# A graph layer on one core: 72 instead of 48 edge columns summed directly, in bf16 addends

## The chip, the cores and the metric

The kernel runs on one core of a Trainium2 chip. The metric is the device time of one execution in microseconds, as a median over runs. The core's engines are TensorE (PE, with its weight loads shown apart as PEld), VectorE (DVE), ScalarE (ACT) and GpSimd (POOL). SyncE (SP) issues transfers. Each engine takes its instructions in one order; they wait for each other through semaphores.

## The reference

There are 6250 nodes and 206,250 edges with 128 features each. `src` and `dst` hold the two ends of every edge, sorted by `dst`. The edge features are summed by `src`, so to the kernel the target of an edge is a random node.

```python
edge_aggr = jnp.zeros((n, HIDDEN)).at[src].add(edge_attr)
combined = jnp.concatenate([x, edge_aggr, global_expand], axis=-1) @ W_c + b_c
h = jax.nn.softplus(combined @ W1 + b1)
h = jax.nn.softplus(h @ W2 + b2)
out = layernorm(x + h @ W3 + b3)
```

The sum over edges, `edge_aggr`, takes nearly all of the time.

## The kernel before, in words

The edges stand as 1612 columns of 128 (the last one is short). A column holds one edge per partition. The sum is built in SBUF, transposed, as `sums_t` (128 features x 6400 nodes), in two ways.

**By scattering (1564 columns).** The columns are cut into ten groups (`GROUPS`, line 23: columns, and `sub`). For each group, `node_codes` (line 205) splits every node number into a block of 256 nodes and a place in the block. `positions` (line 243) counts, with VectorE scans and bf16 matmuls on PE, where each edge goes so that edges of one block lie together in a buffer in DRAM (`place`, three in turn). `load_rows`, `code_rows` and `scatter_rows` (lines 619 to 649) work on pieces of ten columns: SP loads the rows, ScalarE copies each edge's code beside its row (line 636), and POOL scatters each column with one indirect DMA (line 644). `reduce_steps` (line 392) then reads a finished group back in loads of eight chunks of 128 rows. VectorE makes a one-hot matrix `hot` from the codes (line 423; in the last two groups ScalarE does it for three loads in four, lines 414 to 422). PE multiplies (line 437), and VectorE adds the result to `sums_t` (line 454). `sub` chunks share one block and one add.

**Directly (48 columns).** `direct_steps` (line 545) compares the columns with every node. For 12 columns at a time (`SET`) it goes through 13 windows of 512 nodes. A job takes two columns (`QUAD`): ScalarE makes their one-hot rows in two activations and one more (lines 577 and 579), and PE multiplies in fp32 (line 589). At the end of a window, after six jobs, VectorE adds the PSUM result to `sums_t` (line 593).

**The order of the work** is written out by hand for PE, DVE, ACT and SP (lines 652 to 739). While group g is scattered, piece by piece, the steps of four lists are woven in evenly: the positions of group g+1 (done by 75% of the group), the reduction of group g-1 (by 95%), steps of the node part, and the filling of the next buffer. Direct jobs go into groups 1 to 6, shared out by `left` (line 690). All transfers keep one order as well. Lines 713 to 715 issue the rows of the third piece ahead, the codes of the second piece ahead and the scatter of the piece itself, so POOL follows what the other engines reach in their order.

**The end.** After the last reduction, an MLP runs over 13 tiles of 512 nodes. `norm` (line 814) normalises several tiles together: a Newton iteration of short VectorE operations, then a scaling of each 128-node block, on POOL or, for the last part, on VectorE. The tiles are cut into `parts` of 4, 3, 3, 2 and 1 (lines 745 to 748).

Of the kernel before, what the change touches and what calls it, by code (L numbers as in the profile page):

```python
# [16 lines left out]
P = 128  # L17
# [2 lines left out]
LOAD_COLS = 10  # L20
EPS = 1e-5

GROUPS = ((40, 1), (120, 2), (200, 4), (240, 4), (240, 4), (240, 4), (212, 4), (140, 2), (88, 2),
          (44, 1))
CHUNK_ROWS = 1024
PLACES = 3

DIRECT = 48
SET = 12
WIDE = 512  # L30
QUAD = 2
FILL = 4
POS_COLS = 20
PART_COLS = 60
# [6 lines left out]
LEAD = 3  # L41
# [6 lines left out]
def kernel(  # L48
# [36 lines left out]
    for size, sub in GROUPS:  # L85
        c1 = min(TC, c0 + size)
        if c1 > c0:
# [10 lines left out]
    dram = ctx.enter_context(tc.tile_pool(name="dram", bufs=1, space=bass.MemoryType.DRAM))  # L98


    iota_f = const.tile([P, WIDE], F32, name="iota_f")
    nc.gpsimd.iota(iota_f, pattern=[[1, WIDE]], base=0, channel_multiplier=0,
                   allow_small_or_imprecise_dtypes=True)
    part_f = const.tile([P, 1], F32, name="part_f")
    nc.gpsimd.iota(part_f, pattern=[[0, 1]], base=0, channel_multiplier=1,
# [62 lines left out]
    with ExitStack() as phase:  # L168
# [74 lines left out]
        def positions(g):  # L243
# [3 lines left out]
            steps = []  # L247
            parts = [(a, min(c1, a + PART_COLS)) for a in range(c0, c1, PART_COLS)]
            in_block, so_far, got = {}, {}, {}
            pos = per.tile([P, C_MAX], I32, name="pos")  # L250
            pos_of[g] = pos

            def by_col(t):
# [100 lines left out]
            def chunk_map():  # L354

                small = ps.tile([P, 4, P], F32, name="small", bufs=2)
                end_t = per.tile([NB, 1], F32, name="end_t")
                nc.tensor.transpose(small[:NB, 0, :], got["end"], ident)
                nc.vector.tensor_copy(end_t, small[:NB, 0, :1])
                ended = per.tile([NB, NSC_MAX], F32, name="ended")  # L360
                nc.vector.tensor_scalar(ended[:, :nsc], chunk_i[:, :nsc], end_t, None,
                                        op0=ALU.is_ge)
                offs = per.tile([1, NSC_MAX], I32, name="offs", bufs=3)
                offs_of[g] = offs
                flat = ps.tile([P, 4, P], F32, name="small", bufs=2).rearrange("p a b -> p (a b)")
                nc.tensor.matmul(flat[:1, :nsc], ones[:NB, :1], ended[:, :nsc],
                                 start=True, stop=True)
                nc.vector.tensor_scalar(offs[:, :nsc], flat[:1, :nsc], float(NB - 1), float(BL),
                                        op0=ALU.min, op1=ALU.mult)
# [22 lines left out]
        def reduce_steps(g):  # L392
# [16 lines left out]
            def match(i):  # L409
                s, k = loads[i]  # L410
                m = k * sub
                hot = hots.tile([P, CHUNK_ROWS // P, BL], F32, name="hot")
                hot_of[i] = hot
                if g > G - 3 and i % 4 != 3:

                    codes = iota_f[:, int(code_of(g)):int(code_of(g)) + BL]
                    for j in range(m):
                        nc.scalar.activation(hot[:, j], codes, AF.Abs,  # L418
                                             bias=chunks[i][:, j, D:W], scale=-1.0)
                    nc.scalar.activation(hot[:, :m], hot[:, :m], AF.Relu, bias=ones[:, :1],  # L420
                                         scale=-1.0)
                    return
                nc.vector.scalar_tensor_tensor(  # L423
                    hot[:, :m], chunks[i][:, :m, D:W].to_broadcast([P, m, BL]),
                    code_of(g), iota_ps.unsqueeze(1).to_broadcast([P, m, BL]),
                    op0=ALU.subtract, op1=ALU.is_equal)
# [118 lines left out]
        def direct_steps():  # L545


            steps = []
            if not ND:
                return steps  # L550
            NW = -(-NB * BL // WIDE)
            less = keep.tile([P, NW, ND], F32, name="less")
            rows_in, hot_of, sum_of = {}, {}, {}

            def begin():

                first = keep.tile([P, NW], F32, name="first")
                nc.gpsimd.iota(first, pattern=[[WIDE, NW]], base=0, channel_multiplier=0,
                               allow_small_or_imprecise_dtypes=True)
                part, node, _ = whole_nodes(0, ND)  # L560
                nc.vector.tensor_copy(node, part)
                nc.vector.tensor_tensor(
                    less, node.unsqueeze(1).to_broadcast([P, NW, ND]),
                    first.unsqueeze(2).to_broadcast([P, NW, ND]), op=ALU.subtract)

            def load(c):
                n = min(SET, ND - c)
                rows_in[c] = direct_p.tile([P, SET, D], F32, name="direct_rows", bufs=2)
                sync_dma(rows_in[c][:, :n],
                         edge_attr[:P * T, :].rearrange("(p t) d -> p t d", p=P)[:, c:c + n, :])  # L570

            def compare(c, w, q):
                n = min(WIDE, NB * BL - w * WIDE)
                hot = direct_p.tile([P, QUAD, WIDE], F32, name="direct_hot", bufs=4)
                hot_of[c, w, q] = hot
                for j in range(QUAD):
                    nc.scalar.activation(hot[:, j, :n], iota_f[:, :n], AF.Abs,  # L577
                                         bias=less[:, w, c + q + j:c + q + j + 1], scale=-1.0)
                nc.scalar.activation(hot[:, :, :n], hot[:, :, :n], AF.Relu, bias=ones[:, :1],  # L579
                                     scale=-1.0)  # L580

            def add(c, w, q):
                n = min(WIDE, NB * BL - w * WIDE)
                k = min(SET, ND - c)
                hot = hot_of.pop((c, w, q))
                if q == 0:
                    sum_of[c, w] = ps.tile([P, WIDE], F32, name="direct_sum", bufs=2)
                for j in range(QUAD):
                    nc.tensor.matmul(sum_of[c, w][:, :n], rows_in[c][:, q + j, :], hot[:, j, :n],  # L589
                                     start=(q + j == 0), stop=(q + j == k - 1))  # L590
                if q + QUAD == k:
                    here = sums_t[:, w * WIDE:w * WIDE + n]
                    nc.vector.tensor_add(here, here, sum_of.pop((c, w))[:, :n])  # L593

            jobs = [(c, w, q) for c in range(0, ND, SET) for w in range(NW)
                    for q in range(0, min(SET, ND - c), QUAD)]
            steps += [begin, lambda: load(0)]
            for i in range(len(jobs) + 2):
                def one(i=i):
                    if i < len(jobs):  # L600
                        c, w, q = jobs[i]
                        if (w, q) == (NW // 2, 0) and c + SET < ND:
                            load(c + SET)
                        compare(*jobs[i])
                    if i > 1:
                        add(*jobs[i - 2])
                steps.append(one)
            return steps
# [23 lines left out]
        def code_rows(i):  # L632
            if i >= len(pieces):
                return
            g, c, k, r = pieces[i]
            nc.scalar.copy(rows_at[i][:r, :k, D:W], low[:r, c:c + k].unsqueeze(2))  # L636

        def scatter_rows(i):
            g, c, k, r = pieces[i]
# [12 lines left out]
        with tc.manual_schedule(engines={ET.PE, ET.DVE, ET.Activation, ET.SP}):  # L652
# [35 lines left out]


            left = [0.0] * G  # L690
            for g in range(1, G - 3):
                left[g] = max(0.0, groups[g][1] - groups[g][0]
                              - groups[g - 1][3] * groups[g - 1][2] / 3 - (9 if 3 <= g < 6 else 0))
            direct_at = 0.0
            i = 0
            assert G > 6
            nodes = []
            for g in range(G):
                mine = [q for q in range(len(pieces)) if pieces[q][0] == g]
                prep = []  # L700
                if g + 1 < G:
                    prep = [lambda g=g: node_codes(*groups[g + 1][:2])] + positions(g + 1)
                sums = reduce_steps(g - 1) if g else []

                if g == 3:
# [4 lines left out]
                filled = fill_rows(g + 1)  # L710
                done = [0, 0, 0, 0]
                for q in mine:
                    load_rows(i + LEAD)
                    code_rows(i + LEAD - 1)
                    scatter_rows(i)
                    i += 1

# [26 lines left out]

    tiles = [(n0, min(4 * P, N - n0)) for n0 in range(0, N, 4 * P)]
    order = tiles[-1:] + tiles[:-1]
    parts = [order[:4]] + [order[i:i + 3] for i in range(4, len(order) - 3, 3)]
    parts += [order[len(parts) * 3 + 1:-1], order[-1:]]
    h1, h2, sub_z, x_of = {}, {}, {}, {}

    def blocks(w):
# [62 lines left out]
    def norm(now, last):  # L814
# [9 lines left out]
        for _ in range(3):  # L824
            nc.vector.tensor_mul(t, g, g)
            nc.vector.scalar_tensor_tensor(t, t, -0.5, v, op0=ALU.mult, op1=ALU.mult)
            nc.vector.scalar_tensor_tensor(g, t, 1.5, g, op0=ALU.add, op1=ALU.mult)  # L827

        engine = nc.vector if last else nc.gpsimd
        for n0, w, y, at in now["done"]:  # L830
            for lo, hi, r in blocks(w):
                for q in range(lo, hi):
                    engine.tensor_scalar(y[:r, q, :], y[:r, q, :], mv[:r, at + q, 0:1],  # L833
                                         rs[:r, 1, at + q:at + q + 1],
                                         op0=ALU.subtract, op1=ALU.mult)
                m0 = n0 + lo * P
                sync_dma(
                    out[m0:m0 + (hi - lo) * r, :].rearrange("(b p) d -> p b d", p=r),
# [58 lines left out]
```

## Time and profile before

| what | value |
|---|---|
| median of 3 runs | 2163.2 us (2162.69 to 2173.22) |
| profiled execution | 2166.67 us, span 2164.9 us |
| first to last scatter on POOL | 25.6 to 2019.3 us |
| from the last scatter to the first MLP matmul | 66.7 us |
| from there to the end | 78.9 us |
| busy: PE, DVE, ACT, POOL | 1789.7, 1328.0, 912.7, 1560.2 us |
| mean granted clock of PE | 0.925 |

In a group's row of the profile, "out<-in xcount" is followed by the busy time, the mean duration of one instruction in nanoseconds, and the idle time of the engine before them with what ended it. An fp32 matmul appears as two instructions. Matmuls overlap, so the time of one is read from the starts of neighbours rather than from its duration. The chain follows the work that ended last back from the end.

### The profile page before, as it was taken

How to read it: one execution, taken by the hardware profiler on the slowest of the kernel's cores; microseconds unless marked ns; L12 is line 12 of the kernel's file. 1: busy time of each engine (PE TensorE's matmuls, PEld its weight loads, DVE VectorE, ACT ScalarE, POOL GpSimd, SP SyncE). 2: the span in 40 equal slices, each digit the busy share in tenths (PEclk: the TensorE clock that was granted, in tenths of full speed). 3: DMA queues.
4: the chain of work that ended last, by engine and by line, in shares of the span. 5: the costliest groups of instructions: out<-in, count | busy, mean ns of one | idle time of the engine just before them, and what ended most of it. 6: DMA issues, size and time to landing. Idle time of an engine off the chain costs nothing.

```text
span 2164.9 us, 22230 instructions
## 1 busy us (share of the span) xinstructions
PE 1789.7 (83%) x6415; PEld 1209.0 (56%) x6415; DVE 1328.0 (61%) x1923; ACT 912.7 (42%) x1350; POOL 1560.2 (72%) x1631
## 2 busy tenths in 40 slices
PE   3398788966889878999889998788998899688884
PEld 0144445534555555666556666556666778566752
DVE  7386457524656345675465855355755798796567
ACT  0476665653444335444353443353342000006964
POOL 5777777777777767777777777777777777777226
PEclk8699999987999999999999999999999999899997
DMA  9998788738786665676756666556766687776521
GB/s 299 303 313 270 216 256 251 231 101 262 213 225 189 194 193 148 188 207 188 198 173 180 194 190 175 169 167 189 202 198 170 211 245 227 214 213 199 151 75 60
DMA packets 415376, 435.50 MB, mean 201 GB/s; under 512 B 37743, under 2 KB 305766, under 8 KB 415254
## 3 DMA queue, kind: packets, MB, share of 16 engines
q1 hardware_dynamic: 365062, 330.71, 54.9%
q0 software_dynamic: 50048, 103.35, 14.4%
q8 instruction: 51, 0.84, 0.2%
q14 instruction: 71, 0.58, 0.1%
q10 hardware_dynamic: 144, 0.02, 0.0%
HBM read 260.90 MB, written 173.03 MB: 200 GB/s over the span
## 4 chain that ended last, share of the span: by engine, by line
PE 57%; DVE 15%; POOL 9%; issue 7%; DMA 6%; ACT 4%; DVEq 1%; SPq 0%; POOLq 0%; ACTq 0%
PE part L437 37%; PE direct_sum L589 16%; POOL place L644 8%; DVE hot L423 7%; DMA place<-rows,pos 4%; DVE sums_t L454 2%; ACT hot L418 2%; DVE so_far L316 1%; DVE sums_t L593 1%; DMA rows<-in_edge_attr 1%; DMA chunks<-place 1%; PE small L339 1%; POOL y L833 1%; DVEq L448 1%; DVE pos L350 1%
## 5 line engine op out<-in xcount | busy, mean ns | idle before, releaser
L644 POOL DMA_INDIRECT place<-rows,pos x1564 | 1503.2, 961 | 509.0 <-issue 443.5
L437 PE MATMUL part<-hot,chunks 128*128 128x256 f32 x4472 | 1106.0, 405 | 267.8 <-DVE hot L423 250.9
L437 PEld LDWEIGHTS part<-hot,chunks 128*128 128x128 f32 x4472 | 894.9, 203 | 507.8 <-DVE hot L423 310.5
L577 ACT ACTIVATE direct_hot<-iota_f,less 128x512 f32<-128x512 f32 (+1 forms) x624 | 404.6, 695 | 811.0 <-PE direct_sum L589 808.1
L423 DVE SCALAR_TENSOR_TENSOR hot<-chunks,iota_ps 128x2048 f32<-128x2048 f32 (+1 forms) x261 | 592.2, 2270 | 44.2 <-DMA chunks<-place 44.2
L589 PE MATMUL direct_sum<-direct_hot,direct_rows 128*128 128x512 f32 (+1 forms) x1248 | 559.0, 580 | 29.4 <-DMA direct_rows<-in_edge_attr 25.6
L454 DVE TENSOR_TENSOR sums_t<-sums_t,part 128x256 f32 x781 | 327.1, 419 | 133.3 <-PE part L437 110.8
L589 PEld LDWEIGHTS direct_sum<-direct_hot,direct_rows 128*128 128x128 f32 x1248 | 233.3, 190 | 232.2 <-issue 204.9
L579 ACT ACTIVATE direct_hot<-direct_hot,ones 128x1024 f32<-128x1024 f32 (+1 forms) x312 | 348.0, 1115 | 10.1
L593 DVE TENSOR_TENSOR sums_t<-sums_t,direct_sum 128x512 f32<-128x512 f32 (+1 forms) x52 | 34.7, 667 | 410.5 <-PE direct_sum L589 410.5
L636 ACT COPY rows<-src_i 128x10 f32<-128x10 f32 (+1 forms) x159 | 30.7, 196 | 360.3 <-DMA place<-rows,pos 328.9
L350 DVE TENSOR_REDUCE pos<-at 128x20 int32<-128x500 f32 (+2 forms) x80 | 87.0, 1087 | 2.7
L316 DVE TENSOR_TENSOR_SCAN so_far<-iota_ps,ib 128x1500 bf16<-128x1500 f32 (+5 forms) x29 | 85.7, 2955 | 0.0
L418 ACT ACTIVATE hot<-iota_f,chunks 128x256 f32<-128x256 f32 x156 | 64.2, 493 | 26.7 <-DMA chunks<-place 24.2
L845 POOL TENSOR_TENSOR x_sb<-x_sb,b_all 128x512 f32<-128x512 f32 (+1 forms) x13 | 15.2, 1219 | 67.8 <-DMA x_sb<-in_x 67.8
L348 DVE TENSOR_TENSOR at<-small,ib 128x500 f32<-128x500 f32 (+2 forms) x80 | 52.9, 661 | 4.2 <-PE small L339 3.5
L833 POOL TENSOR_SCALAR y<-y,mv,rs 128x128 f32<-128x128 f32 (+1 forms) x45 | 35.2, 796 | 19.9 <-DVE rs L827 19.0
L262 DVE TENSOR_TENSOR ib<-block,iota_ps 128x1500 bf16<-128x1500 bf16 (+5 forms) x29 | 44.2, 1550 | 0.0
L273 PE MATMUL small<-ib,ones_h 128*128 128x500 bf16 (+2 forms) x80 | 23.8, 406 | 23.9 <-DVE ib L262 23.9
L536 DVE TENSOR_SCALAR z_x<-small,z_bias 128x512 f32<-128x512 f32 (+1 forms) x13 | 9.3, 718 | 51.3 <-PE small L534 51.3
L335 PE MATMUL small<-so_far,ones_h 128*128 128x500 bf16 (+2 forms) x80 | 31.4, 393 | 11.1 <-DVE last L319 11.1
L420 ACT ACTIVATE hot<-hot,ones 128x2048 f32<-128x2048 f32 (+1 forms) x20 | 39.2, 1960 | 0.7
(115 smaller groups left out, 472.7 us busy)
## 6 DMA issues: line engine op xcount, KB each, us to landing
chunks<-place SPq DMA_DIRECT2D x278, 516.0 KB, 4.5
rows<-in_edge_attr SPq DMA_DIRECT2D x155, 640.0 KB, 6.7
place<-fill SPq DMA_DIRECT2D x252, 258.0 KB, 8.3
place<-rows,pos POOLq DMA_INDIRECT x1564, 4.5
x_sb<-in_x SPq DMA_DIRECT2D x24, 256.0 KB, 4.6
direct_rows<-in_edge_attr SPq DMA_DIRECT2D x4, 768.0 KB
out<-y SPq DMA_DIRECT2D x12, 256.0 KB, 2.2
chunks<-place SPq DMA_DIRECT2D x3, 258.0 KB, 3.2
```

What stands on the lines that cost most here:

```text
L316: nc.vector.tensor_tensor_scan(t, iota_ps[:, 1:2].to_broadcast([P, NB * n]), in_block[k][0], 0.0, op0=ALU.mult, op1=ALU.add)
L350: nc.vector.tensor_reduce(pos[:, a - c0 + j0:a - c0 + j1], at.rearrange("p b g -> p g b"), axis=mybir.AxisListType.X, op=ALU.add)
L418: nc.scalar.activation(hot[:, j], codes, AF.Abs, bias=chunks[i][:, j, D:W], scale=-1.0)
L423: nc.vector.scalar_tensor_tensor(hot[:, :m], chunks[i][:, :m, D:W].to_broadcast([P, m, BL]), code_of(g), iota_ps.unsqueeze(1).to_broadcast ...
L437: nc.tensor.matmul(part[:, s - q, :], t[:, s * sub + j, :D], hot[:, s * sub + j], start=(j == 0), stop=(j == sub - 1))
L454: nc.vector.tensor_add(here, here, part[:, s - q, :])
L577: nc.scalar.activation(hot[:, j, :n], iota_f[:, :n], AF.Abs, bias=less[:, w, c + q + j:c + q + j + 1], scale=-1.0)
L579: nc.scalar.activation(hot[:, :, :n], hot[:, :, :n], AF.Relu, bias=ones[:, :1], scale=-1.0)
L589: nc.tensor.matmul(sum_of[c, w][:, :n], rows_in[c][:, q + j, :], hot[:, j, :n], start=(q + j == 0), stop=(q + j == k - 1))
L593: nc.vector.tensor_add(here, here, sum_of.pop((c, w))[:, :n])
L644: s = nc.gpsimd.indirect_dma_start(out=dst, out_offset=bass.IndirectOffsetOnAxis(ap=at, axis=0), in_=rows[:r, j, :], in_offset=None)
L833: engine.tensor_scalar(y[:r, q, :], y[:r, q, :], mv[:r, at + q, 0:1], rs[:r, 1, at + q:at + q + 1], op0=ALU.subtract, op1=ALU.mult)
```

## The change

Four parts. First, 72 columns are summed directly. Their fp32 values are split exactly into three bf16 addends: VectorE takes the upper half of each number, then the upper half of the rest, then what is left. PE multiplies three bf16 matmuls per column and window in place of one fp32 matmul. The one-hot rows become bf16, with three buffers in place of four. The first load of direct rows comes a little earlier. Second, the groups after the sixth are cut anew: 178, 116, 84, 44, 24 and 14 columns in place of 212, 140, 88 and 44, and the last four have `sub` 1. ScalarE's one-hot work covers the last four groups (`TAIL`), and in the last three POOL copies the codes itself (`late`). Third, from group 5 on the positions are computed two groups ahead (`SOONER`). Fourth, the last three MLP tiles share one norm, whose scaling is split between VectorE and ScalarE.

```diff
-GROUPS = (... (212, 4), (140, 2), (88, 2), (44, 1))
+GROUPS = (... (178, 4), (116, 2), (84, 1), (44, 1), (24, 1), (14, 1))
+SOONER = 5
+TAIL = 4
-DIRECT = 48
+DIRECT = 72
+SPLIT = 2
...
-            pos = per.tile([P, C_MAX], I32, name="pos")
+            pos = per.tile([P, C_MAX], I32, name="pos", bufs=3)
...
-                if g > G - 3 and i % 4 != 3:
+                if g >= G - TAIL and i % 4 != 3:
...
+            def halves(t):
+                return [t.bitcast(BF16).rearrange("p c (d h) -> p c d h", h=2)[:, :, :, h]
+                        for h in (0, 1)]
+
+            def split(c):
+                n = min(SET, ND - c)
+                less = less_of[c] = direct_p.tile([P, NW, SET], F32, name="less", bufs=2)
+                nc.vector.tensor_tensor(
+                    less[:, :, :n], node_f[:, c:c + n].unsqueeze(1).to_broadcast([P, NW, n]),
+                    first.unsqueeze(2).to_broadcast([P, NW, n]), op=ALU.subtract)
+                low_in[c] = direct_p.tile([P, SET, D], BF16, name="direct_low", bufs=2)
+                for a in range(0, min(SET, ND - c), SPLIT):
+                    b = min(a + SPLIT, SET, ND - c)
+                    rest = direct_p.tile([P, SPLIT, D], F32, name="direct_rest")[:, :b - a]
+                    x_c = rows_in[c][:, a:b]
+                    nc.vector.tensor_sub(rest, x_c, halves(x_c)[1])
+                    nc.vector.tensor_sub(low_in[c][:, a:b], rest, halves(rest)[1])
+                    nc.vector.tensor_copy(halves(x_c)[0], halves(rest)[1])
...
-                hot = direct_p.tile([P, QUAD, WIDE], F32, name="direct_hot", bufs=4)
+                hot = direct_p.tile([P, QUAD, WIDE], BF16, name="direct_hot", bufs=3)
...
-                for j in range(QUAD):
-                    nc.tensor.matmul(sum_of[c, w][:, :n], rows_in[c][:, q + j, :], hot[:, j, :n],
-                                     start=(q + j == 0), stop=(q + j == k - 1))
+                for j in range(q, q + QUAD):
+                    addends = halves(rows_in[c][:, j:j + 1]) + [low_in[c][:, j:j + 1]]
+                    for i, part in enumerate(addends):
+                        nc.tensor.matmul(sum_of[c, w][:, :n], part[:, 0], hot[:, j - q, :n],
+                                         start=(j == 0 and i == 0), stop=(j == k - 1 and i == 2))
...
-            steps += [begin, lambda: load(0)]
+            steps += [lambda: load(0), begin, lambda: split(0)]
...
                         if (w, q) == (NW // 2, 0) and c + SET < ND:
                             load(c + SET)
+                        if (w, q) == (NW - 2, 0) and c + SET < ND:
+                            split(c + SET)
...
-            nc.scalar.copy(rows_at[i][:r, :k, D:W], low[:r, c:c + k].unsqueeze(2))
+            copy = nc.gpsimd.tensor_copy if late(i) else nc.scalar.copy
+            copy(rows_at[i][:r, :k, D:W], low[:r, c:c + k].unsqueeze(2))
+
+        def late(i):
+            return i < len(pieces) and pieces[i][0] > G - TAIL
...
-                if g + 1 < G:
-                    prep = [lambda g=g: node_codes(*groups[g + 1][:2])] + positions(g + 1)
+                for k in range(g + 1 + (g > SOONER), min(G, g + 2 + (g >= SOONER))):
+                    prep += [lambda k=k: node_codes(*groups[k][:2])] + positions(k)
...
                     load_rows(i + LEAD)
-                    code_rows(i + LEAD - 1)
+                    if not late(i + LEAD - 1):
+                        code_rows(i + LEAD - 1)
+                    if late(i):
+                        code_rows(i)
                     scatter_rows(i)
...
-    parts = [order[:4]] + [order[i:i + 3] for i in range(4, len(order) - 3, 3)]
-    parts += [order[len(parts) * 3 + 1:-1], order[-1:]]
+    parts = [order[:4]] + [order[i:i + 3] for i in range(4, len(order), 3)]
...
+                    if last and q % 2:
+                        nc.scalar.activation(y[:r, q, :], y[:r, q, :], AF.Identity,
+                                             bias=minus[:r, k:k + 1], scale=g[:r, k:k + 1])
+                        continue
```

More of the change, by code (lines that the diff above doesn't have):

```diff
@@ L21 @@
 EPS = 1e-5
-GROUPS = ((40, 1), (120, 2), (200, 4), (240, 4), (240, 4), (240, 4), (212, 4), (140, 2), (88, 2),
-          (44, 1))
+GROUPS = ((40, 1), (120, 2), (200, 4), (240, 4), (240, 4), (240, 4), (178, 4), (116, 2), (84, 1), (44, 1),
+          (24, 1), (14, 1))
+SOONER = 5
+TAIL = 4
 CHUNK_ROWS = 1024
 PLACES = 3
-DIRECT = 48
+DIRECT = 72
 SET = 12
@@ L98 @@
     dram = ctx.enter_context(tc.tile_pool(name="dram", bufs=1, space=bass.MemoryType.DRAM))
-    iota_f = const.tile([P, WIDE], F32, name="iota_f")
-    nc.gpsimd.iota(iota_f, pattern=[[1, WIDE]], base=0, channel_multiplier=0,
+    iota_f = const.tile([P, TAIL * BL], F32, name="iota_f")
+    nc.gpsimd.iota(iota_f, pattern=[[1, TAIL * BL]], base=0, channel_multiplier=0,
                    allow_small_or_imprecise_dtypes=True)
@@ L362, in chunk_map @@
                                         op0=ALU.is_ge)
-                offs = per.tile([1, NSC_MAX], I32, name="offs", bufs=3)
+                offs = per.tile([1, NSC_MAX], I32, name="offs", bufs=4)
                 offs_of[g] = offs
@@ L551, in direct_steps @@
             NW = -(-NB * BL // WIDE)
-            less = keep.tile([P, NW, ND], F32, name="less")
-            rows_in, hot_of, sum_of = {}, {}, {}
+            node_f = keep.tile([P, ND], F32, name="node_f")
+            first = keep.tile([P, NW], F32, name="first")
+            less_of = {}
+            rows_in, low_in, hot_of, sum_of = {}, {}, {}, {}
             def begin():
-                first = keep.tile([P, NW], F32, name="first")
                 nc.gpsimd.iota(first, pattern=[[WIDE, NW]], base=0, channel_multiplier=0,
                                allow_small_or_imprecise_dtypes=True)
[L560 to L564, printed above, removed]
+                part, _, _ = whole_nodes(0, ND)
+                nc.vector.tensor_copy(node_f, part)
             def load(c):
@@ L577, in compare @@
                     nc.scalar.activation(hot[:, j, :n], iota_f[:, :n], AF.Abs,
-                                         bias=less[:, w, c + q + j:c + q + j + 1], scale=-1.0)
+                                         bias=less_of[c][:, w, q + j:q + j + 1], scale=-1.0)
                 nc.scalar.activation(hot[:, :, :n], hot[:, :, :n], AF.Relu, bias=ones[:, :1],
@@ L690 @@
             left = [0.0] * G
-            for g in range(1, G - 3):
+            for g in range(1, G - TAIL - 1):
                 left[g] = max(0.0, groups[g][1] - groups[g][0]
                               - groups[g - 1][3] * groups[g - 1][2] / 3 - (9 if 3 <= g < 6 else 0))
+            direct_first = direct[:1]
+            direct = direct[1:]
             direct_at = 0.0
@@ L712 @@
                 for q in mine:
+                    if g == 0 and q == mine[-1]:
+                        for step in direct_first:
+                            step()
                     load_rows(i + LEAD)
-                    code_rows(i + LEAD - 1)
+                    if not late(i + LEAD - 1):
+                        code_rows(i + LEAD - 1)
+                    if late(i):
+                        code_rows(i)
                     scatter_rows(i)
@@ L827, in norm @@
             nc.vector.scalar_tensor_tensor(g, t, 1.5, g, op0=ALU.add, op1=ALU.mult)
-        engine = nc.vector if last else nc.gpsimd
+        if last:
+            minus = work.tile([P, 16], F32, name="minus")[:, :nb]
+            nc.vector.scalar_tensor_tensor(minus, mv[:, :nb, 0], -1.0, g,
+                                           op0=ALU.mult, op1=ALU.mult)
         for n0, w, y, at in now["done"]:
@@ L832, in norm @@
                 for q in range(lo, hi):
-                    engine.tensor_scalar(y[:r, q, :], y[:r, q, :], mv[:r, at + q, 0:1],
-                                         rs[:r, 1, at + q:at + q + 1],
-                                         op0=ALU.subtract, op1=ALU.mult)
+                    k = at + q
+                    if last and q % 2:
+                        nc.scalar.activation(y[:r, q, :], y[:r, q, :], AF.Identity,
+                                             bias=minus[:r, k:k + 1], scale=g[:r, k:k + 1])
+                        continue
+                    (nc.vector if last else nc.gpsimd).tensor_scalar(
+                        y[:r, q, :], y[:r, q, :], mv[:r, k, 0:1], g[:r, k:k + 1],
+                        op0=ALU.subtract, op1=ALU.mult)
                 m0 = n0 + lo * P
```

## The prediction

> **What bounds the kernel now.** I read the page's chain and groups first, then the busy time of each engine in each scatter group, then the timeline around the longest PE waits, and last the spacing of bf16 matmuls.
>
> ```profile
> PE 57%; DVE 15%; POOL 9%; issue 7%; DMA 6%; ACT 4%; DVEq 1%; SPq 0%; POOLq 0%; ACTq 0%
> ...
> L644 POOL DMA_INDIRECT place<-rows,pos x1564 | 1503.2, 961 | 509.0 <-issue 443.5
> L437 PE MATMUL part<-hot,chunks 128*128 128x256 f32 x4472 | 1106.0, 405 | 267.8 <-DVE hot L423 250.9
> ...
> L577 ACT ACTIVATE direct_hot<-iota_f,less 128x512 f32<-128x512 f32 (+1 forms) x624 | 404.6, 695 | 811.0 <-PE direct_sum L589 808.1
> ...
> L579 ACT ACTIVATE direct_hot<-direct_hot,ones 128x1024 f32<-128x1024 f32 (+1 forms) x312 | 348.0, 1115 | 10.1
> L593 DVE TENSOR_TENSOR sums_t<-sums_t,direct_sum 128x512 f32<-128x512 f32 (+1 forms) x52 | 34.7, 667 | 410.5 <-PE direct_sum L589 410.5
> ```
>
> POOL scatters without a pause: 0.961 us and 0.30 of issue, one each 1.265 us, from 25.6 to 2019.3. So it looks like the bound; yet the chain is 57% PE, and PE waits 250.9 us for VectorE's `hot`. In the next view a row is one scatter group (groups 1 to 6, those with direct work); the columns are length, then busy time and instructions of PE, PE's weight load, DVE, ACT and POOL, then the granted PE clock.
>
> ```profile
> 81.20:232.80 151.60, 129.96 (x372) 63.16 (x372) 91.95 (x147) 107.52 (x144) 115.34 (x120) 0.96 0.95 276
> 232.80:485.90 253.10, 203.06 (x636) 121.89 (x636) 132.22 (x185) 147.59 (x206) 192.19 (x201) 0.91 0.73 217
> 485.90:789.60 303.70, 246.57 (x840) 165.47 (x841) 156.87 (x182) 117.60 (x168) 230.59 (x241) 0.88 0.73 209
> 789.60:1102.30 312.70, 279.74 (x985) 187.56 (x983) 183.42 (x215) 135.11 (x186) 230.61 (x240) 0.95 0.67 190
> 1102.30:1405.90 303.60, 264.64 (x966) 181.78 (x966) 181.51 (x215) 127.71 (x183) 230.51 (x240) 0.96 0.63 181
> 1405.90:1675.30 269.40, 240.63 (x878) 167.72 (x879) 161.35 (x194) 107.20 (x154) 203.65 (x212) 0.97 0.64 184
> ```
>
> PE is 80 to 90% busy here, and its clock falls below 1 wherever it paused. How much slack is left? I paired ScalarE's n-th copy of codes (L636) with the n-th piece of ten scatters: the copy stood 45 us ahead of its scatter at the start of group 2, 48 at group 3, then 2, 5, 11 and 13 at the starts of groups 4 to 7. All engines but POOL follow one written order, so that order passed the six starts at 188, 438, 788, 1098, 1395 and 1662, and needed 250, 350, 310, 297 and 267 us for groups 2 to 6. POOL alone needs 253, 304, 304, 304 and 268. **The ordered engines are as slow as POOL; the stage has two bounds, and no slack after group 3.** What they lose time to:
>
> ```profile
> 677.26 0.69 DVE L593 TENSOR_TENSOR sums_t<-sums_t,direct_sum 128x512 f32<-128x512 f32 x1 [14.04 <-PE direct_sum L589]
> 677.87 0.67 DVE L348 TENSOR_TENSOR at<-small,ib 128x500 f32<-128x500 f32 x1
> 678.57 1.10 DVE L350 TENSOR_REDUCE pos<-at 128x20 int32<-128x500 f32 x1
> ...
> 679.58 2.29 DVE L423 SCALAR_TENSOR_TENSOR hot<-chunks,iota_ps 128x2048 f32<-128x2048 f32 x1
> ...
> 681.93 4.63 PE L437 MATMUL part<-hot,chunks 128*128 128x256 f32 x10 [4.70 <-DVE hot L423]
> ```
>
> At each closing of a 512-node window VectorE stands in L593 until PE has finished the window; only then does it make the next `hot`, and PE has nothing to do: 4.70 us here. Closings and PE waits come in pairs through the groups.
>
> **The change, part by part.** *Fewer scatters*: 24 x 1.265 = 30.4 us off POOL. *More direct work*: a job (two columns, one window) is four fp32 matmul instructions at 0.43 us = 1.72 us of PE now (901.86 to 903.58 in PE's timeline); it becomes six bf16 ones. The trace has bf16 matmuls of nearly that size, each with its own weight load:
>
> ```profile
> 903.58 0.38 PE L334 MATMUL small<-ib,upto_h 128*128 128x500 bf16 x1
> 903.79 0.37 PE L335 MATMUL small<-so_far,ones_h 128*128 128x500 bf16 x1
> 904.01 0.37 PE L336 MATMUL small<-more,ones_h 128*128 128x500 bf16 x1
> 904.31 0.38 PE L339 MATMUL small<-begin,scale_h 2*128 2x500 bf16 x1
> ```
>
> They start 0.21 to 0.22 us apart (0.30 where the moving operand is broadcast), so a job is 6 x 0.2155 = 1.29 us. Here a rule of the Trainium skill speaks otherwise: TensorE: Matmul & The Clock Gate, section Back-to-back issue gap, gives about 131 ns for a matmul of 512 columns in a stream with weight loads. By it a job is 0.79 us and 403 jobs (groups 2 to 6) cost 202 us less than by the row. I take the row: same engine, same kernel. 312 jobs become 468. Counted in the two orders, group by group: jobs 42, 64, 58, 53, 53, 44 become 67, 100, 92, 82, 83, 46. With sums, positions and node steps at their durations PE's work changes by +16, +16, +21, +11, +22, -18 us. (Group 5 also takes the positions of group 7; group 6 is 34 columns shorter for POOL, not for PE.)
>
> *More closings*: 52 become 78. For each I took VectorE's work from L593 to the next match less PE's work in between: for groups 2 to 6 that gives 22, 43, 16, 21, 28 us now (measured PE gaps 36, 72, 33, 37, 31, with 9 and 24 of the first two waiting for the first transfer) and 28, 41, 41, 37, 29 in the new order: +6, -1, +25, +16, +1. *Clock*: the same page, section Part 1: The HAM clock gate, says the clock halves after an idle window of 3.4 us and returns after a busy one. The trace agrees in kind: 0.88 where the 4.7 us gaps lie, 0.97 in group 6. Applied to the new gaps that is -8, +8, +10, +6 us in groups 3 to 6; without the rule, nothing. It speaks against the change.
>
> *ScalarE*: a job stays 2 x 0.65 + 1.115, or 2.41 us. 64 jobs of group 1, after PE's first matmul, last 154 us of ScalarE: the order starts group 2 at about 218 (its first copy stands two pieces ahead), not 188: +30. bf16 output alone saves nothing. Three `hot` buffers instead of four cost nothing from group 3 on, where a job comes every 3.3 to 3.7 us; in group 2 (2.5 us apart) up to 15, inside the range.
>
> *Splitting*: per 12 columns 19 VectorE operations, 12 of them two-input ones like L199 (0.37 at 200 elements, so 0.42 at 256), 6 copies at about 0.3, one `less`: 7 us. It stands one job ahead of a closing, so VectorE has no lead to cover it; half shows: 5 x 3 = +15. *Early direct load*: it now passes one load of rows on SP; 768 KB at 300 GB/s, +2.6 us of POOL before group 2, +0 behind a stage bound by PE.
>
> Group 3 loses 20 us of waiting for its first transfer, as the order no longer runs ahead. Sum for the order: 30 + 22 - 8 + 44 + 48 - 11 + 15 = +140, so it passes the start of group 7 at 1662 + 140 = 1802, POOL 4 us later at 1806. POOL alone would be there at 84 + 1218 x 1.265 = 1625: **it waits 181 us, against about 9 now.** Positions two groups ahead don't help: POOL is held by codes and rows, which stand in the order of ScalarE and SP.
>
> *After group 7's start*: 282 columns x 1.265 = 356.7. Eleven copies now on POOL: between a POOL iota of 13 elements (0.14) and ScalarE's copy plus issue (0.5), near the latter: +4. *Tail*: the last 262 128-row chunks all have sub 1. The last group now, also sub 1, took 41.0 us for 68 chunks (2043.0 to 2084.1), 0.603 each; 262 take 158, starting 9 us after group 8's last scatter, while 82 columns and the copies take 108: 58 us from the last scatter to the MLP, against 66.7. *Shared norm*: one Newton chain of 12 short VectorE operations (2148.27 to 2150.95) goes, twelve normalisations are split over two engines instead of eight on POOL and four on VectorE: -2, of a stage of 78.9.
>
> 1806 + 356.7 + 4 + 58 + 76.9 = 2302 us of span. The profiled execution had 2164.9 of span (2166.67 in all), the median of the runs is 2163.2; taking the same 1.7 off gives **2300**.
>
> **Rivals.** *PE's waits do not multiply* (two jobs after a closing hide the match, the split is covered): the order gains only 30 + 16 + 1 + 11 + 22 - 18 = 62, POOL's group 7 starts at 1728, the end is at 2222. For it: with more jobs between matches PE has more cover. Against: the count above already takes that cover off.
> *Faster*: PE's job is far cheaper than the row says, as the skill's 131 ns would have it. Then POOL alone is the bound: 2164.9 - 30.4 + 2.6 + 4 - 8.7 - 2 = 2130, or 2129. It decides at the place where the order must pass group 7 by 1665: 137 us less over 403 jobs, 0.34 a job, a spacing under 0.16 us. Against it stand three rows at 0.21.
> *Weight loads show*: the halves are read with a step of two elements; if that spaces the matmuls as L339's 0.305, 403 x 6 x 0.09 = 217 more, 2516. Against: fp32 loads of 0.19 us hide behind 0.215 now.
>
> **How the numbers follow.** Main case 0.60 (own range 2240 to 2370), waits not multiplied 0.20, faster 0.13, weight loads 0.05, between these (no change) 0.02. Range 2190 to 2390: it leaves out faster, no change and weight loads, 0.20 together. A difference under 0.5% can't be told from none. Faster 0.13, same 0.02, slower 0.85.
>
> **What would show it.** POOL scatters no longer each 1.265 us in groups 2 to 6: some 150 us of waits for ScalarE's copies or rows; group 7 starts near 1800; L437 waits for VectorE's `hot` about 60 us longer; direct matmuls 0.21 apart; the first group's jobs at ScalarE's 2.4 us. Wrong if POOL keeps its pace through group 5, or if VectorE no longer stands in the window's add.

## The result, and the profile after

The changed kernel takes 2300.6 us (median of 4 runs, 2294.0 to 2304.9). Beside it the kernel before took 2163.5 us. The ratio is 1.062, with a 95% interval of 1.058 to 1.066. The forecast was 2300 us.

These are the chain and the groups of the changed kernel that answer to the rows shown of before.

```profile
PE 55%; DVE 18%; DMA 8%; ACT 7%; issue 5%; POOL 4%; SPq 1%; DVEq 1%; ACTq 0%; POOLq 0%
...
L682 POOL DMA_INDIRECT place<-rows,pos x1540 | 1477.5, 959 | 676.7 <-issue 421.2
L443 PE MATMUL part<-hot,chunks 128*128 128x256 f32 x4476 | 1125.9, 410 | 248.6 <-DVE hot L429 226.2
...
L605 ACT ACTIVATE direct_hot<-iota_f,less 128x512 bf16<-128x512 f32 (+1 forms) x936 | 604.9, 693 | 631.6 <-PE direct_sum L619 629.1
L619 PE MATMUL direct_sum<-direct_hot,direct_rows 128*128 128x512 bf16 (+1 forms) x1872 | 540.5, 372 | 100.0 <-ACT direct_hot L607 64.9
...
L607 ACT ACTIVATE direct_hot<-direct_hot,ones 128x1024 bf16<-128x1024 bf16 (+1 forms) x468 | 521.9, 1115 | 15.2
...
L623 DVE TENSOR_TENSOR sums_t<-sums_t,direct_sum 128x512 f32<-128x512 f32 (+1 forms) x78 | 52.0, 667 | 516.2 <-PE direct_sum L619 515.8
```

POOL has 24 scatters fewer, at the same 959 ns. Yet it now idles 676.7 us, against 509.0 before, and its share of the chain fell from 9% to 4%. VectorE stands 515.8 us before the window's add, against 410.5. The chain of waits says whom POOL waits for; its columns are the time in all, how often, and the longest wait.

```profile
POOL place L644 <- ACT rows L636: 12.3, 7, 9.3
...
POOL place L682 <- ACT rows L670: 189.0, 50, 13.2
```

The first row is the kernel before, the second the changed one. The wait grew by 177 us, a little more than the loss of 137 us and the 30.4 us of spared scatters together.

Groups 1 to 6 of the changed kernel, in the same columns as the stages of before:

```profile
86.00:237.60 151.60, 124.58 (x518) 63.39 (x519) 95.58 (x156) 130.17 (x173) 115.30 (x120) 0.98 1.00 275
237.90:516.30 278.40, 230.32 (x1004) 134.98 (x1003) 151.91 (x230) 231.84 (x323) 192.53 (x200) 0.95 0.72 201
516.60:855.50 338.90, 279.86 (x1190) 180.90 (x1190) 175.06 (x223) 217.14 (x297) 230.04 (x240) 0.93 0.68 190
864.40:1197.80 333.40, 282.89 (x1225) 188.00 (x1224) 188.56 (x233) 195.97 (x269) 229.89 (x240) 0.95 0.61 169
1205.30:1543.40 338.10, 288.81 (x1268) 191.59 (x1266) 206.52 (x274) 194.87 (x268) 230.23 (x240) 0.95 0.57 162
1545.30:1799.30 254.00, 227.06 (x977) 164.29 (x977) 148.52 (x180) 117.09 (x162) 170.42 (x178) 0.94 0.64 178
```

POOL is busy for the same 230 us in each group of 240 columns, but such a group now lasts 333 to 339 us instead of 304 to 313. Between some rows lie stretches in which POOL stood before a group's first scatter, 19 us in all. With them, the time from group 2's first scatter to group 7's grew from 1442.5 to 1561.8 us, by 119. PE's busy time grew by 87 us of these (1234.9 to 1321.9), its idle time by 32 (207.6 to 239.9). POOL's group 7 starts at 1799.7, against 1675.6 before.

### The profile page after: what moved, and what is told of

It reads as the page before. It is cut to its first block, busy times and chain, and to the rows that moved or that the text cites. A ratio compares the mean times of both kernels' runs of the same rounds, so it can differ in the third digit from the quotient of the medians.

```text
span 2303.1 us, 26251 instructions
## 1 busy us (share of the span) xinstructions
PE 1884.3 (82%) x7985; PEld 1254.2 (54%) x7985; DVE 1417.7 (62%) x2201; ACT 1302.7 (57%) x1869; POOL 1530.4 (66%) x1610
## 4 chain that ended last, share of the span: by engine, by line
PE 55%; DVE 18%; DMA 8%; ACT 7%; issue 5%; POOL 4%; SPq 1%; DVEq 1%; ACTq 0%; POOLq 0%
PE part L443 37%; PE direct_sum L619 14%; DVE hot L429 7%; DVE sums_t L460 5%; DMA place<-rows,pos 4%; POOL place L682 4%; DMA place<-fill 3%; ACT direct_hot L605 3%; ACT direct_hot L607 2%; SPq L151 1%; DVE sums_t L623 1%; DVE so_far L322 1%; DMA chunks<-place 1%; ACT hot L424 1%; DVE pos L356 1%
## 5 line engine op out<-in xcount | busy, mean ns | idle before, releaser
L682 POOL DMA_INDIRECT place<-rows,pos x1540 | 1477.5, 959 | 676.7 <-issue 421.2
L443 PE MATMUL part<-hot,chunks 128*128 128x256 f32 x4476 | 1125.9, 410 | 248.6 <-DVE hot L429 226.2
L443 PEld LDWEIGHTS part<-hot,chunks 128*128 128x128 f32 x4476 | 902.0, 206 | 460.4 <-DVE hot L429 264.5
L605 ACT ACTIVATE direct_hot<-iota_f,less 128x512 bf16<-128x512 f32 (+1 forms) x936 | 604.9, 693 | 631.6 <-PE direct_sum L619 629.1
L619 PE MATMUL direct_sum<-direct_hot,direct_rows 128*128 128x512 bf16 (+1 forms) x1872 | 540.5, 372 | 100.0 <-ACT direct_hot L607 64.9
L429 DVE SCALAR_TENSOR_TENSOR hot<-chunks,iota_ps 128x2048 f32<-128x2048 f32 x255 | 578.5, 2270 | 2.0 <-DMA chunks<-place 2.0
L607 ACT ACTIVATE direct_hot<-direct_hot,ones 128x1024 bf16<-128x1024 bf16 (+1 forms) x468 | 521.9, 1115 | 15.2
L623 DVE TENSOR_TENSOR sums_t<-sums_t,direct_sum 128x512 f32<-128x512 f32 (+1 forms) x78 | 52.0, 667 | 516.2 <-PE direct_sum L619 515.8
L619 PEld LDWEIGHTS <-direct_rows 128*128 128x128 bf16 x1872 | 180.2, 98 | 310.0 <-issue 106.8
L619 PE MATMUL direct_sum<-direct_hot,direct_low 128*128 128x512 bf16 (+1 forms) x936 | 347.7, 371 | 0.0
L619 PEld LDWEIGHTS <-direct_low 128*128 128x128 bf16 x936 | 91.5, 98 | 103.4 <-issue 1.1
L356 DVE TENSOR_REDUCE pos<-at 128x20 int32<-128x500 f32 (+3 forms) x80 | 85.5, 1068 | 2.7
L322 DVE TENSOR_TENSOR_SCAN so_far<-iota_ps,ib 128x1500 bf16<-128x1500 f32 (+7 forms) x29 | 84.5, 2912 | 0.0
L354 DVE TENSOR_TENSOR at<-small,ib 128x500 f32<-128x500 f32 (+3 forms) x80 | 52.2, 652 | 5.4 <-PE small L345 4.8
```

The costliest lines, as they stand in the source:

```text
L322: nc.vector.tensor_tensor_scan(t, iota_ps[:, 1:2].to_broadcast([P, NB * n]), in_block[k][0], 0.0, op0=ALU.mult, op1=ALU.add)
L354: nc.vector.tensor_mul(at, got.pop((k, j0)), in_block[k][1][:, :, j0:j1])
L356: nc.vector.tensor_reduce(pos[:, a - c0 + j0:a - c0 + j1], at.rearrange("p b g -> p g b"), axis=mybir.AxisListType.X, op=ALU.add)
L429: nc.vector.scalar_tensor_tensor(hot[:, :m], chunks[i][:, :m, D:W].to_broadcast([P, m, BL]), code_of(g), iota_ps.unsqueeze(1).to_broadcast ...
L443: nc.tensor.matmul(part[:, s - q, :], t[:, s * sub + j, :D], hot[:, s * sub + j], start=(j == 0), stop=(j == sub - 1))
L605: nc.scalar.activation(hot[:, j, :n], iota_f[:, :n], AF.Abs, bias=less_of[c][:, w, q + j:q + j + 1], scale=-1.0)
```

## The experiments

Two theories stood against each other. The first is that of the prediction: PE, DVE, ACT and SP follow one written order, that order became slower than POOL, and what makes it slow is PE's added work together with VectorE standing in the window's add. The rival: the new resources cost the time, that is, three one-hot buffers instead of four, and the splitting.

### Four parts of the changed kernel, one at a time

A fourth buffer for the one-hot rows (one buffer of `x_t`, used by the node part, makes room):

```diff
-x_ts[b0] = per.tile([P, 4 * P], F32, name="x_t")
+x_ts[b0] = per.tile([P, 4 * P], F32, name="x_t", bufs=1)
-hot = direct_p.tile([P, QUAD, WIDE], BF16, name="direct_hot", bufs=3)
+hot = direct_p.tile([P, QUAD, WIDE], BF16, name="direct_hot", bufs=4)
```

> The changed kernel with four buffers of one-hot rows in place of three (room for it from a single x_t buffer). PE waits 54 us in groups 2 to 6 for ScalarE's one-hot rows, a wait that was nearly absent before. Theory (the written order is too long because of PE's work and the closings): at most half of that wait goes, 2275 to 2300 us. Rival (ScalarE, held by three buffers, is the cause): the wait and what follows from it go, 2240 us or less.

The window's add written three jobs later, when PE has long finished the window:

```diff
 if q + QUAD == k:
-    here = sums_t[:, w * WIDE:w * WIDE + n]
-    nc.vector.tensor_add(here, here, sum_of.pop((c, w))[:, :n])
+    closing.append((c, w, n))
+if q == 2 * QUAD or (c + SET >= ND and w == NW - 1 and q + QUAD == k):
+    close()      # the same two lines, for each window in `closing`
```

> The changed kernel with the add of a finished window written three jobs later, so that VectorE no longer stands in it. Theory, with closings as a large term: PE's waits for VectorE's matches in groups 2 to 6, 180 us now, fall below 80, the half clock with them, and the order loses 100 to 150 us: 2150 to 2200 us. Rival (PE's own work is all that makes the order long; the waits would only move elsewhere): above 2270 us.

48 direct columns, with all other parts of the change kept (bf16 addends, short last groups, positions, norm):

```diff
-(178, 4), ... DIRECT = 72
+(202, 4), ... DIRECT = 48
```

> The changed kernel with 48 direct columns again (group 6 gets the 24 back), all other parts kept. Theory: the order is as long as before the change or shorter, POOL keeps its 1.265 us per scatter to group 7, which starts at 1655 to 1670, and 503 us follow: 2158 to 2175 us. Rival (the bf16 form itself, with its splits, or the new copies on POOL slow the kernel): above 2200 us.

No splitting: VectorE's three operations on each pair of columns go, the upper half of each number is multiplied three times, and the two lower addends are left out of the sums. Of this edit the diff shows the matmuls' part.

```diff
-addends = halves(rows_in[c][:, j:j + 1]) + [low_in[c][:, j:j + 1]]
+addends = [halves(rows_in[c][:, j:j + 1])[1]] * 3
```

> The changed kernel without the splitting on VectorE: the upper half of each value is multiplied three times, so PE does the same work and the sums are left inexact. Theory (half of the 7 us per split shows): 10 to 25 us less, 2275 to 2290 us. Rival (VectorE's bursts are the main cause): 60 us less or more, 2240 us or below.

| kernel | time, us | POOL's group 7 starts | POOL waits for ScalarE's copies |
|---|---|---|---|
| changed | 2300.6 | 1799.7 | 189.0 |
| four one-hot buffers | 2270.6 | 1767.5 | 156.8 |
| add three jobs later | **2127.2** | 1625.3 | 0.6 |
| 48 direct columns | 2162.2 | 1658.0 | 5.0 |
| no splitting | 2291.9 | 1786.8 | 178.8 |

The four variants ran once each, beside 2163.6 us of the kernel before; the changed kernel's own four runs lie 11 us apart. The fourth buffer is worth 30 us and the splitting about 9, which one run can hardly tell from nothing, so the resources don't carry the loss. With 48 columns all of it is gone (2162.2): the other parts together come out at nothing, and the 24 columns cost 138 us although they take 30.4 us of scatters off POOL. The late add alone brings 173 us, and its group 7 starts at 1625.3, the time the prediction gave for POOL alone (1625). Only the run with 48 columns fell into the range that the first theory named. The fourth buffer gained 4 us more than its range, the missing splits 2 us less, and the late add 23 us more; all three lie nearer to that theory than to the rival.

The two timelines show why. The first is the changed kernel at a closing; the columns are the start, the length, the instruction, and the idle time ahead of it with what ended it. PE's weight loads and some rows are left out.

```profile
959.69 0.38 PE L619 MATMUL direct_sum<-direct_hot,direct_low 128*128 128x512 bf16 x1
...
960.10 1.33 ACT L605 ACTIVATE direct_hot<-iota_f,less 128x512 bf16<-128x512 f32 x2 [2.27 <-PE direct_sum L619]
960.10 0.69 DVE L623 TENSOR_TENSOR sums_t<-sums_t,direct_sum 128x512 f32<-128x512 f32 x1 [10.07 <-PE direct_sum L619]
...
960.71 2.28 DVE L429 SCALAR_TENSOR_TENSOR hot<-chunks,iota_ps 128x2048 f32<-128x2048 f32 x1
...
963.04 3.72 PE L443 MATMUL part<-hot,chunks 128*128 128x256 f32 x16 [2.03 <-DVE hot L429]
```

VectorE, with the next one-hot tile still to make, stands 10.07 us in the add until PE's last direct matmul; then PE stands 2.03 us until that tile is made. The second is the version with the late add:

```profile
953.28 0.69 DVE L616 TENSOR_TENSOR sums_t<-sums_t,direct_sum 128x512 f32<-128x512 f32 x1
...
953.67 0.38 PE L627 MATMUL direct_sum<-direct_hot,direct_rows 128*128 128x512 bf16 x1
953.89 2.28 DVE L429 SCALAR_TENSOR_TENSOR hot<-chunks,iota_ps 128x2048 f32<-128x2048 f32 x1
```

Here the add waits for nothing, and the tile is made while PE multiplies the next window. Over groups 2 to 6, VectorE stands 129.1 us before the add instead of 486.5.

### The late add again, and in the kernel before

> The changed kernel with each window's add written three jobs later, once more for an interval: the last time the kernel before itself took 2863.5 us on that chip, with PE's weight loads standing 480.8 us for nothing that the profile names. Where the kernel before takes its 2163 us, the ratio should be 0.983 (0.980 to 0.986). Where the engines stand as they did then, the written order is the bound in both kernels, and the 68 us of PE work that 24 columns add should make it slower: 1.02 to 1.04, as then.

The same edit in the kernel before:

> The kernel before with the deferred add alone, once more. Theory as before: where POOL keeps its pace of 1.265 us in it, 2154 to 2163 us, ScalarE's copies at the start of group 7 more than 30 us ahead of their scatters instead of 13. Rival, that the closings cost the kernel before itself dearly: under 2130 us. Where the engines stand as in the last call: 0.98 again, for there the order is the bound.

Both came as expected for a kernel before of 2163 us. Beside 2162.3 us of the kernel before, on the same chip, the changed kernel with the late add took 2130.0 us (ratio 0.9845, interval 0.9825 to 0.9866), and the kernel before with the late add 2155.5 us (0.9964, 0.9951 to 0.9977). The latter has these waits:

```profile
ACT rows L645 <- DMA place<-rows,pos: 576.7, 84, 18.3
...
DVE hot L423 <- DMA chunks<-place: 311.0, 58, 41.8
```

ScalarE and VectorE now stand waiting for scatters and for scattered rows: the order has run ahead of POOL. The copies stand 34 to 49 us ahead of their scatters at the starts of groups 2 to 7, where before it was 2 to 11 at groups 4 to 7. That gains only POOL's 9 us of waits and costs it nothing: where POOL is the bound, a lighter order is worth nearly nothing. In the changed kernel, with its 24 columns more, the same edit is worth 171 to 173 us. Together the changes beat both kernels, by 32 us against before.

The stages of the changed kernel with the late add are POOL's own 303 us per 240 columns, and PE is busy 91% of them (1258.5 of 1388.7 us in groups 2 to 6, idle 130.2 instead of 239.9). Rows of its groups show what is left:

```profile
L691 POOL DMA_INDIRECT place<-rows,pos x1540 | 1478.1, 960 | 499.4 <-issue 432.8
L443 PE MATMUL part<-hot,chunks 128*128 128x256 f32 x4476 | 1052.3, 390 | 141.9 <-DVE hot L429 112.8
...
L627 PE MATMUL direct_sum<-direct_hot,direct_rows 128*128 128x512 bf16 (+1 forms) x1776 | 519.5, 371 | 100.7 <-ACT direct_hot L607 67.7
```

PE's waits for VectorE's tiles halved (226.2 to 112.8). Those for ScalarE's tiles stayed (64.9 and 67.7); they don't hold up POOL here.

### Six runs on chips where the engines paused

Six runs fell on two chips where the kernel before itself took 2863.5 and 2870.4 us. Its late-add version shows the pauses in the chain of waits:

```profile
ACT direct_hot L577 <- remote: 716.2, 59, 37.5
POOL place L653 <- ACT rows L645: 541.1, 68, 19.6
...
DVE sums_t L454 <- remote: 531.1, 49, 39.2
...
PE part L437 <- issue: 272.9, 179, 12.4
```

"Remote" and "issue" mean that the wait ended with nothing that this core's profile shows; in the run of the same kernel shown above, PE's, VectorE's and ScalarE's instructions have no such wait. A scatter is as long as there (958 and 961 ns). What holds the engines is not known; the DMA packets that bring the instructions take as long as there (0.68 and 0.69 us on average), so these don't tell it. POOL waits 541.1 us for copies, so there the written order is the bound even in this kernel. These runs can be read against each other only.

> The changed kernel with each window's add written three jobs later, as before, for an interval. One look gave 2127.2 us, so the ratio to the kernel before should be 0.983, with an interval that stays under 0.99. If the one look was a lucky one: 1.00.

> The kernel before with the deferred add alone. Theory: the closings cost the written order time there as well, but that order and POOL were level, POOL waited only about 9 us in all, and its scatters set the end, so 2154 to 2163 us, with the copies 30 us and more ahead of their scatters at the start of group 7 instead of 13. Rival, that the closings cost the kernel before itself dearly (its PE waited 250.9 us for the one-hot tiles): under 2130 us, and deferral is no answer to what the change added.

Against the kernel before, the late-add version of the change came to 1.033 (1.026 to 1.041), and the late-add version of before to 0.984 (0.975 to 0.994). Both misses fit the first theory: where the order is the bound, the late add helps the kernel before by 45 us, and the change with its 24 columns costs 119 us (2937.5 against 2818.9) though the add is late in both. That is an explanation after the result; no expectation had it. The gain of the changed version thus hangs on the order being faster than POOL.

The last groups of before (188, 140, 88 and 44 columns) in the late-add version, on both chips:

```diff
-(178, 4), (116, 2), (84, 1), (44, 1), (24, 1), (14, 1)   TAIL = 4
+(188, 4), (140, 2), (88, 2), (44, 1)                     TAIL = 2
```

> The same, but with the four last groups of the kernel before (188, 140, 88 and 44 columns, ScalarE copying all codes) in place of the six short ones. The scatters are as many. The prediction's step (a tail of 58 us after the last scatter with short groups, 66.7 with long ones, 4 us of copies on POOL) makes this 5 us slower: 2132 us. My reading of the changed kernel's trace (its tail is 68 us, so the short groups shorten nothing, and the copies on POOL cost 4): 2122 us. Short groups worth what their shape suggests (half the last group's reduction, some 20 us): 2145 us or more.

> The deferred version with the four last groups of the kernel before (188, 140, 88 and 44 columns, ScalarE copying all codes) in place of the six short ones, once more. The scatters are as many. The deferred version itself took 2130.0 us. The prediction's step (58 us after the last scatter with short groups, 66.7 with long ones, 4 us of copies on POOL) makes this 5 us slower: 2135 us. The traces read now (66.7 us from the last scatter to the MLP before, 68 after, and 4 us of copies on POOL): 2125 us. Short groups worth half the last group's reduction: 2145 us or more.

They took 2887.4 and 2890.4 us, 1.011 and 1.006 of before; on the first of the two chips that is 50 us less than with short groups. One thing differs from what the expectations say: POOL still copied the codes of the last group (six copies), for its condition goes by `TAIL`, so the copies were not tried apart. The first MLP matmul comes 96.6 us after the last scatter with the long groups and 68.5 with the short ones; but the last scatter comes at 2734 instead of 2793. Neither expectation named this. Nor is the shape of the groups shown to be the reason for the 96.6: the kernel before has long groups too, and takes 67 us there where nothing pauses, and 84 in its late-add version on this chip. What the short groups are worth where nothing pauses is open.

The norm of before in the late-add version (the last tile a part of its own, no share for ScalarE):

```diff
-parts = [order[:4]] + [order[i:i + 3] for i in range(4, len(order), 3)]
+parts = [order[:4]] + [order[i:i + 3] for i in range(4, len(order) - 3, 3)]
+parts += [order[len(parts) * 3 + 1:-1], order[-1:]]
-        if last and q % 2:
+        if False:
```

> The deferred version with the parts and the last normalisations of the kernel before (the last tile a part of its own, its normalisations all on VectorE, the others' on POOL). The prediction's term (the shared norm is worth 2 us): 2129 us. The two traces (from the first MLP matmul to the end 78.9 us before, 71 after): 2135 us.

The total of 2953.2 us can't be told from 2937.5 (1.034, 1.026 to 1.042). The stage itself can: from the first MLP matmul to the end 76.6 us, against 69.3 with the new norm.

The changed kernel with the add in its place and fp32 matmuls for its 72 columns:

```diff
-addends = halves(rows_in[c][:, j:j + 1]) + [low_in[c][:, j:j + 1]]
-for i, part in enumerate(addends): nc.tensor.matmul(..., part[:, 0], hot[:, j - q, :n], ...)
+nc.tensor.matmul(sum_of[c, w][:, :n], rows_in[c][:, j, :], hot[:, j - q, :n], ...)
```

> The changed kernel, with the add where it was, and its 72 columns multiplied in fp32 as in the kernel before: no split, four matmul instructions a job instead of six. The prediction's prices: a job of 1.72 us in place of 1.29, 403 jobs in groups 2 to 6, so 173 us more, less the 9 us of the split that its removal measured: 2465 us. Where the longer jobs take up PE's 65 us of waits for ScalarE's tiles: 2400 to 2420 us. Rival, that PE's direct work lies beside other work and the addends are worth little: under 2340 us.

It took 3004.3 us in one run, 1.047 of before there. The changed kernel did not run on that chip, so the worth of the addends in time is not settled. Only the price of a job is: its fp32 instructions start 0.43 us apart, as in the kernel before, so 1.72 us a job.

## Why the prediction was right, point by point

**Two bounds without slack** was right: 48 columns keep POOL's pace, 72 don't, and with a lighter order POOL has its pace again with either number.

**The length of the order.** The time at which it passed the starts of the groups is read from POOL and from the copies' lead as before:

| | group 1's end | group 2 | 3 | 4 | 5 | 6 | starts group 7 |
|---|---|---|---|---|---|---|---|
| predicted (splitting spread evenly) | 218 | 275 | 345 | 357 | 348 | 259 | 1802 |
| measured | 232 | 282 | 350 | 341 | 340 | 254 | 1799 |

That both end at about 1800 is luck in part. The prediction's start was read 11 us too early: the copy for group 7 stood 3.0 us ahead of its scatter before the change, not 13. (The n-th copy was set against the n-th ten scatters, but group 6 ends with a piece of two.) So the order passed group 7 at 1672.6 us before, and needed 1484.8 us for groups 2 to 6. It now needs 1566.8, which is 82 more and not 110. Group 1 made up for that with 15 us more than forecast, and the part behind group 7's start with 8. These misses nearly cancel; that the order is the bound, and by how many tens of us, is not luck.

**PE's work** was right. These are neighbouring starts in the changed kernel:

```profile
966.60 0.59 PE L619 MATMUL direct_sum<-direct_hot,direct_rows 128*128 128x512 bf16 x2
966.82 0.10 PEld L619 LDWEIGHTS <-direct_low 128*128 128x128 bf16 x1
967.03 0.38 PE L619 MATMUL direct_sum<-direct_hot,direct_low 128*128 128x512 bf16 x1
967.03 0.31 PEld L619 LDWEIGHTS <-direct_rows 128*128 128x128 bf16 x2
967.25 0.59 PE L619 MATMUL direct_sum<-direct_hot,direct_rows 128*128 128x512 bf16 x2
```

A row of two matmuls and one of a single matmul begin 0.43 and 0.22 us apart, so the spacing is 0.215 us as taken from the rows of before, and not the 131 ns of the Trainium skill (TensorE: Matmul & The Clock Gate, section Back-to-back issue gap). The rival on weight loads fell too: those of the halves, read with a step of two, take 98 ns like those of the packed third addend. Between the order's own times for groups 2 to 6, PE's busy time grew by the 52 us of work that the steps gave (1273.0 to 1325.4).

**The closings** were the right place, with the wrong sign in the profile. The steps counted 176 us of stalls for all closings of the new order in groups 2 to 6, 47 of them new. Taking the closings' wait away brought group 7 from 1799.7 to 1625.3, 174 us, and POOL hid more: the copies then stood 21 us ahead. From group 2's first scatter to group 7's, PE's idle time fell by 115 us with it (239.9 to 124.7; before L443 from 179 to 52), and its busy time by 58. The second is the clock: the granted clock in these traces is either 1.00 or 0.50 (0.50 from 682 to 686 us of the kernel before, behind the gap of 4.70 us), and PE worked at 0.50 for 25 us instead of 143. But L443's waits for `hot` over the whole run did not grow by 60 us from before to after, as the prediction had it: they fell from 250.9 to 226.2, and there were 87 of them as against 88, though 78 windows closed and not 52. **The wait it put at nothing** came instead: PE waited 64.9 us for ScalarE's one-hot rows, 51.3 of them in groups 2 to 6 (3.9 before in the whole run), where three buffers were to cost nothing from group 3 on. The fourth buffer brought the order to group 7 32 us earlier: 8 in group 1, 10 in group 2, where the prediction allowed up to 15, and 14 in groups 3 to 6, which that step missed. Between the order's own times PE's idle time grew by 30 us (211.8 to 241.4); the steps for closings, splitting and the spared first transfer gave 47 + 15 - 20, or 42. So the size of this term came out roughly right with the wrong waits in it.

**The rivals.** That waits don't multiply (2222 us) was true of L443's, but the other wait and group 1 filled the gap. For the faster case the spacing would have had to fall under 0.16 us.

**The clock** was wrong: 16 us more were worked out from the gaps. The clock stood at 0.50 for 167 us of groups 2 to 6, against 195 before, but PE worked in only 143 of them, against 141, so the term came to about 1 us.

**ScalarE in group 1** was low: 45 us instead of 30. From the first direct matmul to the copy for group 2 the order took 145 us for 52 jobs, 2.79 us each and not 2.41, for ScalarE waited 18 us for PE in between. With the late add it was 2.60, with 9 us of waits. That copy came 12 us earlier with the late add, 8 with the fourth buffer and 9 without splitting, so no one of them is all of the 15.

**Splitting**: 9 us instead of 15. Its instructions cost what was said (0.42, 0.42 and 0.31 us at 256 elements), but they showed elsewhere. In the run without them, 9 of the 13 us won by group 7 are won before group 2, where the first split stands ahead of the first direct matmul and was counted at nothing; the other five, counted at 15, come to 4. This rests on one run.

**After group 7's start**: 503.4 us instead of 495.6. The scatters took 364.1 (360.7): the eleven copies on POOL cost under 0.1 us each, not 4 in all, but the very last scatter waited for its rows behind SP's reads of finished chunks:

```profile
2152.77 6.10 SPq L151 DMA_DIRECT2D chunks<-place  x2
...
2159.50 0.35 SPq L151 DMA_DIRECT2D rows<-in_edge_attr  x1
...
2162.87 0.90 POOL L682 DMA_INDIRECT place<-rows,pos  x1 [7.15 <-DMA rows<-in_edge_attr]
```

The tail took 68 us, not 58 (66.7 before): the 262 chunks took 0.627 us each and began 13 us after group 8's last scatter instead of 9. So the tail is no shorter than with the long groups of before. The MLP took 71 us, not 76.9: the norm gave 8 us, not 2 (7 in the run with the old norm). The steps took the removed VectorE chain at its own 2.7 us; before, the chain of the part ahead of it also held back the next `h` and PE behind it (PE waited 3.63 us for `h` at 2141.46), and fewer parts mean fewer such places. That last reason is read from the trace and was not tried apart. The positions two groups ahead were not tried apart either.

## What to carry to other kernels

Before work is moved from one engine to others, measure how far the others are ahead: here ScalarE's copies stood 2 to 11 us ahead of the scatters that wait for them, and work taken off POOL and put into the other engines' order could then only cost time. An instruction that collects another engine's result belongs in the order where that result is already there; three jobs later, in two PSUM buffers that existed, was worth 173 us where the order was the bound and 7 where POOL was. The same edit can be worth nothing, a little or all, so it is to be tried again after each change of the bound.

## What the runs showed of the hardware

The same program took 2162 to 2164 us on some chips and 2864 to 2870 on two others, with scatters of the same length (958 to 963 ns in the runs there, 959 to 961 in the others). What the traces show of the difference is pauses that end with nothing in this core's profile: 421 us of idle time before PE's instructions in the late-add version of before end with "issue", none on the other chip. Which of two kernels is the faster turned round with it (0.9845 and 1.033). Reading bf16 halves out of fp32 numbers in place, with a step of two elements, cost TensorE's weight loads nothing: 98 ns either way.
